# A sparse mixture of experts, split into two lots of tokens that are routed and combined beside other work

## The chip, the cores and the metric

The kernel runs on one core of a Trainium2 chip. Its time is the device time of one execution in microseconds (us). The core has a matrix engine (TensorE, called PE in the profile; its weight loads are shown apart as PEld), a vector engine (VectorE, DVE), an activation engine (ScalarE, ACT), a general engine (GpSimd, POOL) and a queue processor that issues most transfers (SyncE, SP). Each engine runs its own instructions in order; semaphores tie the engines together. 16 DMA engines move data between the large memory (DRAM) and the on-chip memory (SBUF); TensorE writes its results to a small accumulator memory (PSUM).

## The reference: what is computed

There are 4096 tokens of 256 numbers (`x`) and a sparse row-normalized 4096 x 4096 matrix (`adj`). Two layers, each made of a propagation over the graph and a mixture of experts:

```
x = x + mamba(layernorm(relu(adj @ layernorm(x) @ gcn_w + gcn_b)))
x = x + sum over the top 2 of 8 experts of w_e * (gelu(h @ W1[e] + b1[e]) @ W2[e] + b2[e])     h = layernorm(x)
f = tanh(adj * adj) * (adj > 0);  keep the 700 largest of each row of f
x = x + relu(f @ (tanh(layernorm(x) @ W_proj + b_proj) @ W_gcn) + b_gcn)
x = x + sum over the top 2 of 6 experts of w_e * expert_e(h)                                   h = layernorm(x)
```

In the last line, the router is a small network (256 to 128, relu, to 6 numbers, softmax); the weights of the two chosen experts are a softmax over their two values. An expert is three layers of 256 x 256 with relu behind the first two. Only two of the six experts count for a token, so the kernel computes only those: 8192 rows (token, expert) instead of 24,576. No row of `adj` in the given inputs has more than 22 entries, so "the 700 largest" keeps all of them.

## The kernel before

**Tokens.** They are held in 8 chunks of 512 (`NC`, `CW`), each 4 groups of 128 (`TPC`, `P`). `x3` is the result of the second propagation, all of it on chip.

**The second propagation** (`propagate1`) makes one chunk of 512 output rows after the other. Per chunk there are 16 steps: load a block of the transposed matrix (SP), relu (DVE, L1344), square and tanh (ACT, L1345, L1346), count the positive entries (DVE), and four matrix products into `pf` (L1355). At the end of the chunk, `pc` sums the counts (L1361), ACT applies relu, TensorE transposes back (`ps_ft`) and DVE adds into `x3`. A callback, `before(j2)`, puts other work between the steps. In chunk 0 it carries the combining of the first mixture and `node_features`; in chunks 1 to 7 it carries the routing of the chunk just finished: `prepare` at step 2, `choose` at step 6.

**Routing a chunk** (`Route`). `prepare` normalizes the chunk, stores the rows to DRAM (`d_xd`), transposes them, applies the router's first layer and computes the logits. `choose` picks the two experts as one-hot rows (`oh`), the two weights (`wv`), and each row's place within its expert (`place`, with running counts from chunk to chunk in `count`); `one_hot` then writes `lo`, a one-hot of the place modulo 128.

**The tables** (`tables`, L257). Rows of one expert are padded to tiles of 256 rows (`TR`), so every tile has one expert. 8192 rows and 6 experts need at most `K` = 37 tiles. `tables` inverts the map from row to place: for every batch of 8 groups DVE makes two one-hots over the `C` = 74 half tiles (`tb_hot`, `tb_eq`), and TensorE multiplies them with `lo` into `ps_inv` (L300; 64 products of 148 columns). From the sums DVE works out, per place, which row to fetch (`src`), the expert of each tile (`exps`), the tile's biases, and where the result goes (`dst`).

**The tiles** (`expert_tiles`, L421). For tile k, SP reads the expert's number into a register (`expert`) and loads three weight matrices (`wk`, three buffers each) and a bias; POOL fetches 2 x 128 rows by index (`xk`, L359, four buffers). TensorE transposes them (`ps_xt`, L465), DVE copies them to `xkT`, and TensorE runs the layers (`ps_h`, L444), with ACT between them (`hk`, L448). The last layer (`ps_y`, L429) of tile k stands behind the first layer of tile k+1; DVE adds the bias (`yk`, L434) and POOL scatters the rows by index to `d_ys` in DRAM (L367).

**Combining** (`combine`, L492). For a chunk, SP loads two blocks of 512 KB from `d_ys` (`yg`, three buffers; token t of group g, one row of 1 KB per partition and group), one with each token's first expert and one with its second. Both loads wait for the last four scatters. DVE does `dst = yg * weight + src` for 4 groups and both blocks (L503). For the second mixture the result goes to `x3`, and SP stores it to `out` (L1493).

**The order before.** After the propagation's 8 chunks, the kernel takes the largest count of a row (`most`) into a register; `If(many > TOPK)` holds an exact row-by-row top-700 and a new routing of 7 chunks, which these inputs don't need. Then come, one after the other: routing of chunk 7, `tables` for all rows, 37 tiles, and the combining of 8 chunks. The first mixture (8 experts) is built by the same functions; it runs 35 tiles, and up to 4 more in a branch of its own when the counts ask for them.

**What sets the order.** The program is written as one sequence; a static scheduler puts it on the engines' queues in that order. Pools of buffers add waits: an instruction that writes a buffer again waits for the last reader of what was in it. So the place of an instruction in the text, and the number of buffers, decide what is queued behind what.

Of the kernel before, what the change touches and what calls it, by code (L numbers as in the profile page):

```python
# [9 lines left out]
F32 = mybir.dt.float32  # L10
# [8 lines left out]
P = 128  # L19
# [4 lines left out]
TOPK = 700  # L24


@with_exitstack
def kernel(ctx: ExitStack, tc: tile.TileContext, out: bass.AP, **a):
# [122 lines left out]
    class Dispatch:  # L151
# [4 lines left out]
        def __init__(self, pool, E, name, batches):  # L156

            self.E, self.pool, self.name, self.T = E, pool, name, batches
            self.t0 = [sum(batches[:b]) for b in range(len(batches))]
            self.K = 2 * N // TR + E - 1  # L160
# [7 lines left out]
            self.xd = dram.tile([N, D], F32, name=f"{name}_xd")  # L168
            self.ys = dram.tile([2 * N + self.K * TR, D], F32, name=f"{name}_ys")
# [3 lines left out]
            self.oh = []  # L173
            for b, T in enumerate(batches):
                t = pool.tile([P, 2 * T + 1, E], BF16, name=f"{name}_oh{b}")
                nc.gpsimd.memset(t[:, :1, :], 0.0)
                self.oh.append(t)
# [8 lines left out]
            for i in range(2):  # L186
                nc.vector.tensor_scalar(
                    self.group[:, :, i], iota[:, :NT], float(i * NT), None, ALU.add
                )
# [12 lines left out]
        def place(self, b, psum, tag, pool):  # L202
# [6 lines left out]
            ps, tot = (psum.tile([P, CW], F32, name=f"ps_pl{i}", tag=tag) for i in range(2))  # L209
# [47 lines left out]
        def tables(self, psum, tp, biases):  # L257


            E, K, C, name = self.E, self.K, self.C, self.name  # L260
            nt = small.tile([P, E], F32, name="tb_nt", bufs=1)
# [10 lines left out]
            self.tiles = self.pool.tile([1, 1], I32, name=f"{name}_tiles")  # L272
            nc.vector.tensor_copy(self.tiles, ct[0:1, 0, E - 1:E])

            ps = psum.tile([P, CW], F32, name="ps_inv", tag="pl")
            group = self.group.rearrange("p t i -> p (t i)")
            shift = tp.tile([P, 2 * NT], F32, name="tb_shift", bufs=1)
            for b, T in enumerate(self.T):
                g0, G = 2 * self.t0[b], 2 * T
                one = tp.tile([P, G, E], F32, name=f"tb_one{G}")  # L280
                nc.vector.tensor_tensor(
                    one, self.oh[b][:, 1:, :], base.to_broadcast([P, G, E]), ALU.mult
                )
                nc.vector.tensor_reduce(shift[:, g0:g0 + G], one, AX.X, ALU.add)
            nc.vector.tensor_tensor(shift, shift, self.hi, ALU.add)
            S = 2 * TPC
            for g0 in range(0, 2 * NT, S):
                eq = tp.tile([P, 2, S, C], BF16, name="tb_eq", bufs=3)
                hot = tp.tile([P, S, C], BF16, name="tb_hot", bufs=3)
# [9 lines left out]
                for g in range(S):  # L299
                    nc.tensor.matmul(  # L300
                        ps[:, :2 * C], self.lo[:, g0 + g, :], eq[:, :, g, :],
                        start=(g0 + g == 0), stop=(g0 + g == 2 * NT - 1),
                    )

            tmp = tp.tile([P, K, E], F32, name="tb_tmp", bufs=1)
# [14 lines left out]
            grp = tp.tile([P, C], I32, name="tb_grp", bufs=1)  # L320
            no = tp.tile([P, C], F32, name="tb_no", bufs=1)
# [3 lines left out]
            nc.vector.tensor_scalar(grp, grp, NT - 1, None, ALU.bitwise_and)  # L325
# [5 lines left out]
            out = []  # L331
            for n, b in enumerate(biases):
# [9 lines left out]
                out.append(bk)  # L342

            nc.vector.scalar_tensor_tensor(
                tok, inv[:, 1, :], float(P), inv[:, 0, :], ALU.mult, ALU.add
            )
            nc.vector.tensor_scalar(tok, tok, -1.0, None, ALU.add)
            nc.vector.tensor_scalar(no, inv[:, 0, :], 0.0, None, ALU.is_equal)
            nc.vector.tensor_scalar(inv[:, 1, :], iota[:, :C], float(P), part1, ALU.mult, ALU.add)
            nc.vector.tensor_scalar(inv[:, 1, :], inv[:, 1, :], float(2 * N), None, ALU.add)  # L350
# [3 lines left out]
            return out  # L354
# [32 lines left out]
    class Route:  # L387
# [9 lines left out]
        def prepare(self, b):  # L397
            dp, E = self.dp, self.dp.E
            xn = self.pool.tile([P, TPC, D], F32, name="xn_r")
            layernorm(self.source[:, b * TPC:(b + 1) * TPC, :], xn)  # L400
# [20 lines left out]
    def expert_tiles(dp, psum, pool, weights, bias_out, layers, kb_out, spare):  # L421
# [3 lines left out]
        def finish(k, w, bk, hT):  # L425
# [25 lines left out]
        def tile_of(k, prev):  # L451
# [18 lines left out]
            for n, (mb, func, bias) in enumerate(layers):  # L470
                hT = layer(ws[n], hT, mb, func, bias[:, :, k:k + 1], f"hk{n}")
                if n == 0 and prev is not None:
                    finish(*prev)
            return k, ws[-1], bk, hT

        def run(first, last):
            prev = None
            for k in range(first, last):
                prev = tile_of(k, prev)
            finish(*prev)  # L480

        if not spare:
            return run(0, dp.K)


        most = 2 * N // TR + dp.E // 2 - 1
        tiles = nc.values_load(dp.tiles[0:1, 0:1], min_val=1, max_val=dp.K)
        run(0, most)
        with tc.If(tiles > most):
            run(most, dp.K)  # L490

    def combine(dp, pool, c, src, dst):  # L492

        yg = []
        for i in range(2):
            yg.append(pool.tile([P, TPC, D], F32, name="yg", bufs=3))
            ld = nc.sync.dma_start(yg[i], tokens(dp.ys, i * NC + c))
            for o in dp.sent[-4:]:
                after(ld, o)
        for t in range(TPC):  # L500
            s_ = c * TPC + t
            for i in range(2):
                nc.vector.scalar_tensor_tensor(  # L503
                    dst[:, s_, :], yg[i][:, t, :], dp.wv[:, s_, i:i + 1], (src, dst)[i][:, s_, :],
# [748 lines left out]
    with ExitStack() as s2:  # L1253
        with ExitStack() as st:
            tp = st.enter_context(tc.tile_pool(name="tiles0", bufs=2, reuse_waits="tile"))
            with ExitStack() as sr:
# [7 lines left out]
                (b1k,) = dp.tables(ps_r, rp, [b1])  # L1264
# [8 lines left out]
            expert_tiles(  # L1273
# [112 lines left out]
        def route_of(c):  # L1386
            def step(j2):
                if j2 == 2:
                    early.prepare(c)
                elif j2 == 6:  # L1390
                    early.choose(c)
# [169 lines left out]
```

## Time and profile before

| | |
|---|---|
| time before, median of 3 | 2511.99 us (2510.48 to 2512.32) |
| the profiled execution's own time | 2536.95 us |
| its span | 2535.2 us |
| TensorE busy, mean granted clock | 2262.7 us (89%), 0.946 |
| VectorE, ScalarE, GpSimd busy | 1652.5, 1194.7, 1137.6 us |
| bytes moved, mean rate | 507.85 MB, 200 GB/s |
| second propagation's last product into `pf` ends | 2193.2 us after the span's start |
| first layer of the first tile starts | 2246.66 |
| last tile's result added (`yk`) | 2485.64 |
| span ends | 2535.2 |

The page describes one execution by the hardware's profiler. A span is the time between its first and last instruction; the execution's own time is the span and a little around it. Engines are counted as busy while they execute, not while they wait. The granted clock is the share of full speed that the chip allowed TensorE in a stretch of time. In a "slices" view the span is cut into 40 equal parts and a digit is the busy share in tenths. In a "windows" view each line is a stretch, with the busy time of the engines, the clock, the share of time that the 16 DMA engines were busy (it may be slightly over 1) and the bytes per second. A "chain" follows the work that ended last from the end backwards, always to what released it. In a "timeline" line: start, duration, engine, line, operation, output <- inputs, shape, and in brackets how long the engine had idled and for what.

### The profile page before, as it was taken

The page shows a single profiled execution, that of the slowest core. Times are in us where ns is not written, and L with a number is a line of the kernel's source. Part 1 is how long each engine was busy: PE and PEld are TensorE (multiplying, and loading weights), DVE is VectorE, ACT ScalarE, POOL GpSimd, SP SyncE. Part 2 cuts the span into 40 slices and gives each one's busy share as a digit, 9 for nine tenths or more (in the row PEclk, how much of TensorE's full clock was granted, in tenths as well). Part 3 has the DMA queues.
Part 4 walks back from the last instruction along what each step waited for, and adds up shares of the span by engine and source line. Part 5 has one row for each costly group of instructions (what it writes and reads, how often), then busy time and mean ns, then how long its engine had stood idle before and what let it go on. Part 6 is the DMA issues. An engine that isn't in the chain of part 4 may idle for free. (4 is left out here: it accounts for less than half of the span.)

```text
span 2535.2 us, 25727 instructions
## 1 busy us (share of the span) xinstructions
PE 2262.7 (89%) x7996; PEld 1448.4 (57%) x7996; DVE 1652.5 (65%) x2324; ACT 1194.7 (47%) x2025; POOL 1137.6 (45%) x831
## 2 busy tenths in 40 slices
PE   5999999899999999897967999699999999769992
PEld 4765655656465656544636888555444444357781
DVE  4049999999999999988983111382666666432224
ACT  1146656574655566575722222244665656322330
POOL 1037676777777777765623555210000000036650
PEclk9989999999999999998978999899999999879996
DMA  6369999989899999996745777541444444147776
GB/s 200 92 179 225 241 271 233 266 227 270 222 271 230 250 256 238 263 244 195 237 148 175 236 229 232 192 150 59 153 151 147 147 148 145 47 146 224 231 228 215
DMA packets 302015, 507.85 MB, mean 200 GB/s; under 512 B 25248, under 2 KB 173728, under 8 KB 300976
## 3 DMA queue, kind: packets, MB, share of 16 engines
q1 hardware_dynamic: 255792, 409.63, 51.6%
q0 software_dynamic: 46080, 96.50, 18.0%
q8 instruction: 67, 1.10, 0.2%
q14 instruction: 76, 0.62, 0.1%
HBM read 404.85 MB, written 42.47 MB: 176 GB/s over the span
## 5 line engine op out<-in xcount | busy, mean ns | idle before, releaser
L1082 POOL TENSOR_TENSOR db<-du,bb 128x1024 f32<-128x1024 f32 x256 | 607.4, 2373 | 355.8 <-ACT state L1103 127.7
L1097 DVE TENSOR_TENSOR_SCAN db<-da,state,db 128x512 f32<-128x512 f32 x512 | 627.4, 1266 | 43.3 <-ACT da L1090 41.0
L621 PE MATMUL pt<-at,gn 128*128 128x256 f32 x2048 | 491.8, 393 | 35.9 <-DMA at<-in_adjT_dram 27.3
L1090 ACT ACTIVATE da<-dt,negA 128x512 f32<-128x512 f32 x512 | 347.8, 691 | 358.4 <-DVE db L1097 356.6
L621 PEld LDWEIGHTS pt<-at,gn 128*128 128x128 f32 x2048 | 400.8, 197 | 167.1 <-issue 74.0
L1355 PE MATMUL pf<-f,gn 128*128 128x512 f32 x1024 | 449.4, 594 | 0.0
L1124 PE MATMUL psy<-hc,ident 128*128 128x512 f32 x576 | 305.4, 624 | 42.6 <-DMA hc<-hc 36.3
L1107 DVE TENSOR_TENSOR hc<-db,cb 128x1024 f32<-128x1024 f32 x256 | 331.3, 1294 | 17.9
L1355 PEld LDWEIGHTS pf<-f,gn 128*128 128x128 f32 x1024 | 191.8, 190 | 227.3 <-issue 225.7
L448 ACT ACTIVATE hk<-ps_h,d_b 128x256 f32<-128x256 f32 x288 | 136.2, 474 | 380.3 <-PE ps_h L444 268.4
L434 DVE TENSOR_TENSOR yk<-ps_y,bk 128x512 f32<-128x512 f32 x72 | 49.8, 692 | 384.9 <-PE ps_y L429 288.7
L78 POOL TENSOR_TENSOR ln_rs<-ln_rs,mhalf 128x4 f32<-128x4 f32 x24 | 34.5, 1437 | 573.2 <-DVE ln_rs L77 573.2
L1345 ACT ACTIVATE f<-f 128x1024 f32<-128x1024 f32 x128 | 135.3, 1057 | 198.7 <-DVE f L1344 176.9
L359 POOL DMA_INDIRECT xk<-d_xd,d_src x144 | 140.2, 973 | 186.5 <-PE ps_xt L465 79.3
L429 PE MATMUL ps_y<-wk,hk 128*128 128x256 f32 x856 | 209.0, 381 | 7.9 <-issue 4.6
L444 PE MATMUL ps_h<-xkT,wk 128*128 128x256 f32 x856 | 209.3, 387 | 2.7 <-issue 2.4
L367 POOL DMA_INDIRECT d_ys<-yk,d_dst x144 | 142.4, 989 | 130.4 <-DVE yk L434 97.2
L1344 DVE TENSOR_SCALAR f<-at 128x1024 f32<-128x1024 f32 x128 | 88.1, 688 | 166.1 <-PE pf L1355 159.4
L1111 POOL DMA_DIRECT2D hc<-hc x224 | 195.5, 873 | 0.2
L1124 PEld LDWEIGHTS psy<-hc,ident 128*128 128x128 f32 x576 | 110.1, 198 | 119.9 <-issue 62.1
L444 PEld LDWEIGHTS ps_h<-xkT,wk 128*128 128x128 f32 x856 | 158.2, 192 | 35.6 <-ACT hk L448 9.4
L429 PEld LDWEIGHTS ps_y<-wk,hk 128*128 128x128 f32 x856 | 159.8, 190 | 30.8 <-issue 6.2
(236 smaller groups left out, 2491.7 us busy)
## 6 DMA issues: line engine op xcount, KB each, us to landing
at<-in_adjT_dram SPq DMA_DIRECT2D x256, 512.0 KB
bb<-bcd SPq DMA_DIRECT2D x128, 512.0 KB
cb<-bcd SPq DMA_DIRECT2D x128, 512.0 KB
hc<-hc POOLq DMA_DIRECT2D x224, 256.0 KB
wk<-in_L_ffn_W_dram SPq DMA_DIRECT2D x70, 512.0 KB
wk<-in_L_ffn_expert_w_dram SPq DMA_DIRECT2D x111, 256.0 KB
yg<-d_ys SPq DMA_DIRECT2D x32, 512.0 KB
yd<-us SPq DMA_DIRECT2D x6, 1024.0 KB
```

Of the source, the lines that this page charges most:

```text
L359: nc.gpsimd.indirect_dma_start(out=xk[:, j, :], out_offset=None, in_=self.xd[:, :], in_offset=bass.IndirectOffsetOnAxis(ap=self.src[:, c:c ...
L367: s_ = nc.gpsimd.indirect_dma_start(out=self.ys[:, :], out_offset=bass.IndirectOffsetOnAxis(ap=self.dst[:, c:c + 1], axis=0), in_=yk[:, j, ...
L429: nc.tensor.matmul(ps[:, j, :], hT[:, m, j * P:(j + 1) * P], w[:, m, :], start=(m == 0), stop=(m == kb_out - 1),)
L444: nc.tensor.matmul(ps[:, j, :], w[:, d, m * P:(m + 1) * P], xT[:, d, :], start=(d == 0), stop=(d == DB - 1),)
L621: nc.tensor.matmul(pt[:, k, :], xl[:, j, k * P:(k + 1) * P], at[:, jj, :], start=(j == 0 and k == 0), stop=(j == NT - 1 and k == DB - 1),)
L1082: nc.gpsimd.tensor_tensor(self.db, self.f.du[self.half][:, self.mi:self.mi + 1, :].to_broadcast([P, 2, CW]), self.bb, ALU.mult,)
L1090: nc.scalar.activation(da, self.f.dt[self.half][:, self.mi, :], AF.Exp, scale=negA[:, self.m, n:n + 1])
L1097: nc.vector.tensor_tensor_scan(self.db[:, j, :], da, self.db[:, j, :], state[:, self.m, n:n + 1], ALU.mult, ALU.add,)
L1107: nc.vector.tensor_tensor(self.hc, self.db, self.cb, ALU.mult)
L1111: nc.gpsimd.dma_start(self.hc[:, 0, :], self.hc[:, 1, :], accum_op=ALU.add)
L1124: nc.tensor.matmul(f.psy[m], ident, self.hc[:, j, :], start=False, stop=(self.g == GS - 1 and j == last),)
L1355: nc.tensor.matmul(pf[:, k, :], gn[:, j, k * P:(k + 1) * P], f[:, jj, :], start=(j == 0), stop=(j == NT - 1),)
```

## The change

The second mixture is done in two lots of tokens: lot a is chunks 0 to 5 (`SPLIT` = 6), lot b is chunks 6 and 7. Each has a `Dispatch` of its own, with its own counts, tables, `d_xd` and `d_ys`.

- Lot a needs at most K = 29 tiles and 27 are run; lot b at most 13, and 11 are run (`few`). That is 38 in place of 37.
- `tables` became a generator that stops after each batch. Lot a's tables are stepped from the callback in the last chunk of propagation, at every step but 2 and 6, where chunk 6 is routed as before. Its one-hots lie in the buffers that held `yg` of the first mixture, its sums in a buffer of `pf`.
- The branch between propagation and mixture is gone.
- A hook, `also(n)`, runs behind tile n of the 38. Behind tiles 1 to 26 it carries a piece each of chunk 7's routing and of lot b's tables, until they are done. Behind tiles 28, 29, 31, 32, 34 and 35 it carries the combining of one of lot a's six chunks and its store. Lot b's two chunks are combined after the last tile.
- `d_ys` has another row order: the four rows of a partition lie beside each other, so a load of `yg` takes 4 KB per partition in one piece. `dst` needs three more steps on DVE for it. The first mixture has this order too.
- A flag is set when a row has over 700 entries or when either lot needs more tiles than were run. `If(again > 0)` at the very end then does everything again in a general way (exact top-700 where it was, routing of 8 chunks, tables, all 37 tiles, combining).
- The one-hots of all batches of one size share a buffer, so `tables` treats them with one instruction each; the per-row offsets are summed from bf16 products.

```diff
+SPLIT = 6
...
-            self.K = 2 * N // TR + E - 1
+            self.NT = NT = sum(batches)
+            self.K = 2 * NT * P // TR + E - 1
...
-            self.ys = dram.tile([2 * N + self.K * TR, D], F32, name=f"{name}_ys")
+            self.S = 1 << (NT // TPC - 1).bit_length()
+            self.ys = dram.tile([2 * self.S * CW + self.K * TR, D], F32, name=f"{name}_ys")
...
-        def tables(self, psum, tp, biases):
+        def tables(self, ps, tp, biases, hots=None):
...
+            yield
             S = 2 * TPC
-            for g0 in range(0, 2 * NT, S):
-                eq = tp.tile([P, 2, S, C], BF16, name="tb_eq", bufs=3)
-                hot = tp.tile([P, S, C], BF16, name="tb_hot", bufs=3)
+            for g0 in range(0, NG, S):
+                eq = hots((P, 3, S, C))
+                hot = eq[:, 2]
...
+                yield
...
-    def expert_tiles(dp, psum, pool, weights, bias_out, layers, kb_out, spare):
+    def expert_tiles(jobs, psum, pool, weights, bias_out, layers, kb_out, also=None):
...
+        prev = None
+        for n, (d, k) in enumerate(jobs):
+            prev = tile_of(d, k, prev)
+            if also is not None:
+                also(n)
+        finish(*prev)
...
             yg.append(pool.tile([P, TPC, D], F32, name="yg", bufs=3))
-            ld = nc.sync.dma_start(yg[i], tokens(dp.ys, i * NC + c))
+            r0 = (i * dp.S + c) * CW
+            ld = nc.sync.dma_start(
+                yg[i], dp.ys[r0:r0 + CW, :].rearrange("(p t) d -> p t d", t=TPC)
+            )
...
         def route_of(c):
+            d = early[c >= SPLIT]
+            table = None
+            if c == NC - 2:
+                table = dp1[0].tables(
+                    ps_f.tile([P, DB, CW], F32, name="pf")[:, 0, :], tb, [eb1, eb2],
+                    lambda shape: wk.tile(list(shape), BF16, name="tb_eq", tag="yg", bufs=3),
+                )
             def step(j2):
                 if j2 == 2:
-                    early.prepare(c)
+                    d.prepare(c - d.dp.c0)
                 elif j2 == 6:
-                    early.choose(c)
+                    d.choose(c - d.dp.c0)
+                elif table is not None:
+                    next(table, None)
             return step
...
-    many = nc.values_load(mosti[0:1, 0:1], min_val=0, max_val=N)
...
-        with tc.If(many > TOPK):
...
+    def to_out(d, b, pool):
+        c = d.c0 + b
+        o = pool.tile([P, TPC, D], F32, name="oc")
+        combine(d, pool, b, x3[:, c * TPC:(c + 1) * TPC, :], o)
+        return nc.sync.dma_start(tokens(out, c), o)
+
+    few = [2 * d.NT * P // TR + E1 // 2 for d in dp1]
...
+        def routing():
+            late.prepare(NC - 1 - SPLIT)
+            yield
+            late.choose(NC - 1 - SPLIT)
+            yield
+            yield from dp1[1].tables(
+                ps_r.tile([P, CW], F32, name="ps_inv", tag="m"), rp, [eb1, eb2]
+            )
+
+        pieces = routing()
+        ready, op = list(range(SPLIT)), []
+
+        def also(n):
+            if n == few[0]:
+                assert next(pieces, None) is None
+                sr.close()
+                op.append(s4.enter_context(tc.tile_pool(name="out1", bufs=2, reuse_waits="tile")))
+            elif n < few[0]:
+                if n > 0:
+                    next(pieces, None)
+            elif (n - few[0]) % 3 != 0 and ready:
+                stores.append(to_out(dp1[0], ready.pop(0), op[0]))
+
+        tiles1([(d, k) for d, f in zip(dp1, few) for k in range(f)], psums, tp, also)
+        for b in range(NC - SPLIT):
+            stores.append(to_out(dp1[1], b, op[0]))
...
+        nc.vector.tensor_scalar(flag, flag, TOPK + 0.5, None, ALU.is_gt)
+        for d, f in zip(dp1, few):
+            nc.vector.scalar_tensor_tensor(flag, d.tiles, f + 0.5, flag, ALU.is_gt, ALU.add)
+        after(nc.vector.tensor_copy(flagi, flag), dp1[1].sent[-1])
+        again = nc.values_load(flagi[0:1, 0:1], min_val=0, max_val=3)
+    with tc.If(again > 0):
...
-            rt.prepare(NC - 1)
-            rt.choose(NC - 1)
-            b1k, b2k = dp1.tables(ps_r, rp, [eb1, eb2])
...
-        for c in range(NC):
-            combine(dp1, op, c, x3, x3)
-            nc.sync.dma_start(tokens(out, c), x3[:, c * TPC:(c + 1) * TPC, :])
```

## The prediction, made before the changed kernel was run

> **What bounds the kernel now.** I read the page's slices first, then the windows, then the chain of waits and the timeline over the last 340 us, where all the large edits lie.
>
> The slices, 63.4 us each; the last six are the second mixture:
>
> ```profile
> PE   5999999899999999897967999699999999769992
> PEclk9989999999999999998978999899999999879996
> DMA  6369999989899999996745777541444444147776
> ```
>
> TensorE is full except in two places near the end: where the second propagation gives way to the mixture (slices 35 and 36) and in the last slice. The windows (stretch, then PE, PEld, DVE, ACT and POOL busy, clock, DMA share, GB/s) show what fills them:
>
> ```profile
> 2131.90:2193.30 61.40, 61.13 (x162) 27.80 (x162) 37.53 (x79) 30.79 (x34) 1.85 (x1) 1.00 0.36 112
> ...
> 2210.00:2222.00 12.00, 0.31 (x2) 0.11 (x1) 10.95 (x65) 0.98 (x3) 0.00 (x0) 0.51 0.00 0
> 2234.00:2246.00 12.00, 1.86 (x6) 0.91 (x6) 5.04 (x20) 0.00 (x0) 7.80 (x9) 0.50 0.97 295
> ...
> 2320.00:2340.00 20.00, 19.95 (x97) 16.68 (x96) 5.44 (x8) 6.17 (x13) 12.57 (x13) 1.00 0.69 235
> ...
> 2504.00:2514.00 10.00, 0.00 (x0) 0.00 (x0) 7.07 (x18) 0.00 (x0) 0.00 (x0) 0.50 1.05 342
> ```
>
> Propagation is bound by PE (61.13 of 61.4) and leaves DVE 24 us a chunk. Then one engine after another works alone: DVE routes and builds tables, POOL starts the fetches, and the DMA queues load weights. In the tiles PE is full. In the tail PE does nothing and DMA is saturated.
>
> The chain names what ended last in the two gaps, and one tile's period between them:
>
> ```profile
> 2195.42 5.60 issue
> 2248.63 5.45 another core or an unknown queue
> 2282.22 1.99 PE ps_h L444 x8
> 2288.26 1.99 PE ps_h L444 x8
> 2490.43 3.95 DMA yg<-d_ys
> 2498.17 5.82 DMA yg<-d_ys
> ```
>
> The timeline gives the edges:
>
> ```profile
> 2193.13 0.59 PE L1361 MATMUL pc<-cnt,ones_b 128*1 128x512 bf16 x2
> 2202.10 1.38 DVE L80 TENSOR_SCALAR xn_r<-x,ln_mv,ln_rs 128x256 f32<-128x256 f32 x4 [1.12 <-POOL ln_rs L78]
> 2225.53 2.00 PE L300 MATMUL ps_inv<-tb_eq,d_lo 128*128 128x148 bf16 x16 [0.58 <-DVE tb_eq L295]
> 2246.66 1.92 PE L444 MATMUL ps_h<-xkT,wk 128*128 128x256 f32 x4
> 2485.64 0.69 DVE L434 TENSOR_TENSOR yk<-ps_y,bk 128x512 f32<-128x512 f32 x1 [3.99 <-PE ps_y L429]
> 2490.43 6.03 SPq L497 DMA_DIRECT2D yg<-d_ys  x4
> 2501.76 0.40 SPq L1493 DMA_DIRECT2D out_dram<-x  x1
> ```
>
> Propagation's last matmul ends at 2193.2, the first tile's first layer starts at 2246.66: a head of 53 us. The last tile's result is added at 2485.64, its scatter lands at 2490.3, the span ends at 2535.2: a tail of 45 us.
>
> **The change part by part**, in us of the profiled execution (span 2535.2, time 2536.95). The median of the runs shown is 2511.99, 25 us less; I carry differences over unscaled (1% of 40 us is 0.4).
>
> *Does the new fixed number of tiles suffice?* Lot a runs 27 tiles, lot b 11, and anything more goes to the general path. I computed the router's choices from the reference's inputs: lot a has 387, 1232, 858, 1845, 1182 and 640 rows, that is 2+5+4+8+5+3 = 27 tiles; lot b has 146, 384, 294, 621, 374 and 229, that is 11. Both fit with nothing to spare. The nearest count that could add a tile is 229, which would need 28 more rows, and the smallest gap between second and third logit is 4e-5, so rounding won't move it.
>
> *1. Lot a's tables inside the last chunk of propagation.* PE gets 48 table matmuls; 16 took 2.00 at 148 columns (now 116), so 6.0 at most, all on the path since PE is full there. DVE gets six pairs of one-hots (0.77 each at 592 columns, now 464, so about 7) and some 12 of small steps, 19 on top of 37.5: 57 in a chunk that now lasts 67. In the built order the last table step stands three matrix pieces before the end, so indices, fetches (six at 1.25) and weights are issued in the last 15 to 25 us of the chunk. The weight loads stand on SP's queue right after the last adjacency load and wait only for the table matmuls, whose buffers they reuse. Taken +6; bounds +4 (fewer columns scale fully) and +12 (DVE falls 6 behind).
>
> *2. The head.* The branch between propagation and mixture goes (x3's add ends at 2196.43, the next statistics start at 2198.95: 2.5), and so does the wait for routing, tables, fetch and weights. What stays on PE's queue, in built order: two tiles' transposes, then transposes of the last chunk's normalized rows, then the first layer. So PE still waits for that layernorm: 2202.10+0.41-2.5 = 2200.0, and starts the first layer about 2201.2. That is 45.5 earlier than 2246.66. Bounds: -47 (it need not wait for the copy) and -36 (it also waits for chunk 7's hidden layer and logits, 2202.66 to 2209.6 now, and the copies between).
>
> *3. Filling.* The first tiles now run at clock 0.66 and wait 5.45 for late weights. With weights there and PE hardly idle: -5 (0 to -6).
>
> *4. The last chunk's routing between tiles.* Chunk 6's same steps ran at full clock in 1.64 (transposes), 1.88, 0.95 and 0.5, plus 16 table matmuls 2.0: +7 of PE work. PE is in order, so it also waits where ACT or DVE is late (four places); behind it queue the tiles' matmuls. Only the exponentials-to-one-hot chain is long (2209.6 to 2213.4), and tile work stands between. Taken +10 (7 to 17).
>
> *5. One tile more.* 37 tiles took 2246.66 to 2485.6, 6.46 each: +6.5 (6.0, the undisturbed period 2282.22 to 2288.26, to 7).
>
> *6. Six chunks combined beside lot b's tiles.* New on SP's queue, ahead of later weights: 12 loads and 6 stores of 512 KB; on DVE 48 steps of 0.48 (3.85 a chunk, where yk and xkT take 1.4 of a tile's 6.04). Bytes: a tile moves 233 GB/s x 6.3 us = 1.47 MB, ten tiles 14.7 MB, the chunks 9.4 MB, 24.1 MB in all. At the tail's 342 GB/s that takes 70 us, at the tile stretch's 235/0.69 also 71; ten tiles take 63. So 8 from bytes. On top, SP stands for the last scatters of lot a and for DVE at each store, with the weights of two tiles ahead behind it; and DVE stands for a load while the next tile's xkT copy is queued behind (by the order I get about 5 for PE once, near lot b's fourth tile). Taken +15. Bounds: 0 (all hidden) and +28.5, six times the 4.75 that a chunk now costs in the tail, as if none of it overlapped.
>
> The Trainium skill (DMA: Bandwidth & Descriptors, Issuing engines are not separate DMA queues) says that DMAs of all issuers end up on the same 16 engines and interleave, so loads moved beside tiles aren't taken off them; and Specifications puts HBM at about 358 GB/s a core. By that figure the 24.1 MB take an estimated 67 us, the bytes' share of this step would be 4 instead of 8, and the whole -44 instead of -40. No row here reaches 358; the highest stretch is 342.
>
> *7. The tail.* Two chunks remain. From the scatter's landing at 2490.3, today's second store is issued at 2501.76 (11.5 later); the last DVE step ends at 2530.8, 4.4 before the end. So 15.9 instead of 44.9: -29. Loads of four rows per partition in one piece may be quicker; nothing shows it. Bounds -31 and -24 (loads at 5.82 rather than 3.95, twice, and a slow store).
>
> *8. The branch at the end* now jumps over the general path. Today's branch costs 2.5 to 5.6; most of it passes while the last store lands. +2 (0 to 5).
>
> *9. First mixture.* Table sums in bf16, three DVE steps more of 0.2, results read in the new row order: 0 (-3, as 16 loads stand at the start of a propagation chunk where PE idles 19.5 for the first; +1).
>
> Sum: 6 - 45.5 - 5 + 10 + 6.5 + 15 - 29 + 2 + 0 = **-40**. All bounds bad: +10.5; all good: -70.
>
> **The rivals.**
> - *More hidden than I think* (chance 0.13): step 6 costs the bytes' 8 or less, step 1 and 4 their lower bounds: 4-47-6+7+6+4-30+1 = -61, 2451. For it: the DMA share of a tile is only 0.69 to 0.78. Against: DVE and SP stand in order.
> - *The head stays half open* (0.14): PE's order puts routing ahead of tiles, DVE is late in the last chunk: 12-36-3+17+6.5+15-29+2 = -15.5, 2496. For it: four in-order waits on short chains. Against: DVE has 10 us to spare.
> - *Combining starves the tiles: slower* (0.09). Place: SP and DVE in lot b. If a chunk costs PE a loaded read (5.82), DVE's 3.25 and the two copies of a tile (1.4), 10.5 each, step 6 is 63 and the sum +8: 2520. It decides from 9.2 us a chunk ((40+15)/6). For it: the DMA share 1.05 in the tail. Against: weights are asked for two tiles (12 us) ahead.
> - *The general path runs* (0.01): at least 37 more tiles, 239 us, besides the row loop; ruled out by the counts unless these are wrong.
>
> **How the numbers follow.** My forecast, -40, has 0.60; 0.03 is left for a sum near nothing. Predicted: 2511.99-40 = 2472. Its own range is 2455 to 2489. To leave out no more than 2 in 10, I take in most of the first two rivals: 2446 to 2500. The measurement of this kernel can tell about 0.2% (5 us). Faster by more: 0.60+0.13+0.14 = 0.87; within: 0.03; slower: 0.09+0.01 = 0.10.
>
> **What would show it.** After: table matmuls among pf's in the last chunk, and that chunk about 67 long; the first ps_h within 10 us of the last pf; no wait of 5 for weights there; 38 tiles; lot b's tiles at 7 to 8 us against 6.0 to 6.5; yg loads of six chunks before the last scatter; the span ending about 16 to 18 after it lands. I'm wrong if lot b's tiles take 10 us or more, if PE idles over 15 us at the head, or if the matmuls of the general path appear.

## The result, and the profile after

The changed kernel takes 2477.72 us (median of 4, 2470.45 to 2479.38) where the kernel before, in the runs that go with it, takes 2512.15 (median of 4, 2510.48 to 2519.68). The ratio is 0.985, with a 95% interval of 0.982 to 0.988: 34 us, or 1.4%, faster. Predicted were 2472, with a range of 2446 to 2500.

One thing has to be known for all that follows. The kernel was later run on three more occasions, on three chips, and the kernel before took 2518.4 us on one of them, 2532.9 on another and 2536.2 on the last. I call them chips A, B and C. Times are therefore compared only with runs of the kernel before on the same chip. The changed kernel itself was run on A and not on B or C; a variant that ran there is set against the ratio of A. That a ratio holds from chip to chip was seen for one kernel only, the variant with "fetched rows in memory of their own" (0.9816 on A, 0.9821 on C). On chip A the two kernels stood side by side: 2477.85 against 2518.36, ratio 0.984 (0.983 to 0.986), 40.5 us. The execution of before that was profiled for the prediction took 2536.95 us, like those on B and C; the one profiled after took 2478.58, like those on A. The spans of these two profiles therefore differ by 58.5 us, more than the change is worth.

The stages, in us, from three profiles of before (the one shown, chip B, chip C) and two of after (the one on record, chip A):

| stage | before | after |
|---|---|---|
| start to the first product into `pf` | 1646.6, 1643.2, 1649.1 | 1651.7, 1650.0 |
| first to last product's end | 546.6, 546.4, 547.5 | 548.1, 549.4 |
| head: to the first tile's first layer | 53.5, 54.3, 54.1 | 11.1, 11.1 |
| to the last tile's result | 239.0, 235.4, 236.7 (37 tiles) | 243.2, 245.7 (38 tiles) |
| tail: to the end | 49.5, 49.1, 49.1 | 22.6, 22.7 |

Head and tail agree within 1 us in all traces of a kernel, and they carry the gain: some 43 and 27 us. The slices of the profile on record show it, 61.9 us each:

```profile
PE   5989989999999999896994999969999999989985
PEclk9989999999999999997996999989999999999998
DMA  6259898999999999988655777743344444447886
```

The first of the two thin places of before is gone: from the 28th slice, where the second propagation starts, no digit of PE is below 8 but the last, which holds the tail. The clock keeps its 9s through the change from propagation to mixture (slice 36), and from the 28th slice on DMA is now busiest in slices 38 and 39, lot b's. The windows of the same profile (stretch, then PE, PEld, DVE, ACT and POOL busy, clock, DMA share, GB/s):

```profile
2132.00:2199.90 67.90, 67.24 (x218) 31.31 (x217) 44.64 (x112) 34.18 (x39) 1.85 (x1) 1.00 0.42 132
2199.90:2211.00 11.10, 4.03 (x20) 2.43 (x19) 5.71 (x19) 1.26 (x2) 7.98 (x8) 0.78 0.29 72
2300.00:2320.00 20.00, 19.95 (x97) 16.67 (x96) 5.44 (x8) 6.32 (x14) 13.33 (x14) 1.00 0.78 240
2380.00:2400.00 20.00, 16.13 (x73) 12.94 (x72) 9.98 (x22) 4.27 (x9) 10.47 (x12) 0.93 0.89 299
2400.00:2420.00 20.00, 16.34 (x69) 13.48 (x69) 8.65 (x19) 4.75 (x11) 8.44 (x10) 0.90 0.94 315
2420.00:2440.00 20.00, 18.01 (x85) 14.14 (x84) 10.40 (x22) 5.69 (x12) 8.07 (x9) 1.00 0.99 323
2455.00:2466.00 11.00, 0.00 (x0) 0.00 (x0) 2.73 (x8) 0.00 (x0) 1.94 (x2) 0.67 0.54 190
```

Line 2 is the head: 11 us, in which PE works for 4. Line 3 is lot a's tiles alone, PE full. Lines 4 to 6 are lot b's tiles with lot a's chunks combined beside them: DMA goes from 0.78 to 0.99 and PE loses 2 to 4 us in every 20. The last line is the start of the tail.

What holds the head at 11 us is seen in the chain of waits of the same profile:

```profile
2199.89 1.28 ACT fT L1408 x2
...
2207.52 0.95 POOL xk L383
...
2208.49 1.07 POOL ln_rs L79
...
2209.58 0.42 DVE xn_r L81
...
2210.05 0.48 PE ps_tr L91
2210.52 0.64 PE ps_xt L491 x3
2211.16 1.71 PE ps_h L470 x4
```

Chunk 7's layernorm has one step on POOL (`ln_rs`), and it stands behind the row fetches of the first three tiles. DVE, then PE's transposes of the normalized rows (`ps_tr`), and behind these the first tile's layer wait for it. The fetches themselves are late. The timeline of POOL:

```profile
2201.16 1.03 POOL L383 DMA_INDIRECT xk<-d1a_xd,d1a_src  x1 [55.59 <-ACT fT L1408]
```

The indices they use are written at 2175.05, 26 us before. The fetch waited for `fT`, the propagation's last use of the memory that `xk` was given.

In lot b, the chain of waits shows both stops that the prediction named:

```profile
2385.57 5.18 DMA yg<-d1a_ys
...
2396.39 0.40 SPq L1470
...
2400.53 9.57 DMA wk<-in_L_ffn_expert_w_dram
...
2432.57 1.67 DVE oc L524 x4
2434.24 0.61 DVE xkT L495
2434.89 1.13 PE ps_h L470 x4
```

SP issues the store of a combined chunk (L1470) when DVE is done with it; the weights of a later tile stand behind it on SP's queue, go out at 2400.53, and need 9.57 us to land on full DMA queues. At 2432.57 the copy `xkT` stands behind a chunk's four combining steps, and PE's layer behind the copy.

### The profile page after: what moved, and what is told of

Its sections match the earlier page's. It is cut to its first block, busy times and chain, and to the rows that moved or that the text cites. A ratio compares the mean times of both kernels' runs of the same rounds, so it can differ in the third digit from the quotient of the medians.

```text
span 2476.7 us, 25809 instructions
## 1 busy us (share of the span) xinstructions
PE 2259.5 (91%) x8024; PEld 1448.7 (58%) x8024; DVE 1652.7 (67%) x2368; ACT 1194.0 (48%) x2029; POOL 1141.4 (46%) x830
## 5 line engine op out<-in xcount | busy, mean ns | idle before, releaser
L470 PE MATMUL ps_h<-xkT,wk 128*128 128x256 f32 x864 | 214.7, 390 | 12.5 <-DVE xkT L495 8.4
L474 ACT ACTIVATE hk<-ps_h,d_b 128x256 f32<-128x256 f32 x140 | 66.2, 474 | 184.2 <-PE ps_h L470 184.2
L1394 DVE SCALAR_TENSOR_TENSOR cnt<-at,cnt 128x1024 bf16<-128x1024 f32 x120 | 146.1, 1217 | 11.6 <-DMA at<-in_adjT_dram 10.5
L754 PE MATMUL ps_xz<-hT,w_in 128*128 128x512 f32 x256 | 126.4, 630 | 14.7 <-ACT hT L742 14.7
```

The lines of the kernel that those rows point to most:

```text
L470: nc.tensor.matmul(ps[:, j, :], w[:, d, m * P:(m + 1) * P], xT[:, d, :], start=(d == 0), stop=(d == DB - 1),)
L1394: nc.vector.scalar_tensor_tensor(cnt, at, 0.0, cnt, ALU.is_gt, ALU.add)
```

## The experiments

The theory was the prediction's: the head falls by the chain that is now hidden, the tail by six chunks, and lot b's tiles pay some 15 us for the combining beside them. The rivals were that combining beside the tiles hides little, that the head's parts cost in their new place what they cost in the old, and that the branch at the end costs more than it seems. All changes below are against the changed kernel, unless said otherwise.

### The changed kernel and the kernel before, again

> The changed kernel itself, measured beside the other variants, on the same chip as they. The runs so far come from two chips: before took 2512 on the one and 2533 on the other. Theory: the ratio to before is the same on both (0.985), so 2475 where before takes 2512, 2495 where it takes 2533, and where before's tiles of 5.2 us take 7.0 (every fifth), the same happens here. Rival: the change's gain is larger where the tiles have these stops: 0.980 or lower.

Chip A: 2477.85 (2477.08 to 2480.81) against 2518.36 for before; ratio 0.9842 (0.9826 to 0.9859). The ratio is the one on record, 0.985. In the trace of before, most results of the second mixture's tiles come 6.0 us after one another, but every fifth some 7.0 us; these are the stops that the expectation speaks of. Here, in lot a's tiles, every fifth result comes after 5.2 us, so the stops of 1.8 us are not there on this chip.

> The kernel before, unchanged, profiled a second time. The profiled execution of before took 2536.95 us where its unprofiled runs took 2512; the two profiles differ by 58.5 us in span, the medians by 34.4. Theory A: that one execution was slow by chance in the mixture's tiles (37 tiles in 239 us, PE idle for 14 of them, waits called issue of 1.2 us in every fifth tile), and a second profile has a span near 2510 to 2515, with its tiles nearer 225. Theory B: the profile itself or the kernel always costs this, and the span is again near 2535 with the same waits; then the runs without a profile differ in a way no trace shows.

Chip B: 2530.14, span 2528.4, and the same stops in every fifth tile. This is nearer to theory B: the stops are no chance of one execution.

> The kernel before once more, for a trace of it where its time is near 2512 to 2518: its two traces so far are from executions of 2530 and 2537. Theory: on such a chip every fifth tile of the second mixture takes 5.2 us as in the traces of the changed kernel there, in place of 7.0, so its 37 tiles take 225 to 230 in place of 235 to 239; head (54) and tail (49) are the same. Rival: the tiles take 235 or more there too, and the 15 us between the chips lie elsewhere.

This came to chip C, 2538.29, with the stops in every fifth tile once more. No trace of before was had on chip A, so the question was not answered directly; the section on the hardware has an answer from another kernel that ran on both A and C.

### Combining at the end, first in the text only, then held there

```diff
-            elif (n - few[0]) % 3 != 0 and ready:
-                stores.append(to_out(dp1[0], ready.pop(0), op[0]))
...
+        for b in range(SPLIT):
+            stores.append(to_out(dp1[0], b, op[0]))
         for b in range(NC - SPLIT):
             stores.append(to_out(dp1[1], b, op[0]))
```

> The changed kernel with one part undone: lot a's six chunks are combined after the last tile, followed by lot b's two. My theory (combining beside tiles hides most of it, step 6 against step 7 of the prediction): the tiles of lot b lose the stops that the trace of after shows (PE idle for 10.3 of 71.3 us), so -7 to -10, and the tail grows by six chunks at 4.75, +28.5; together +18 to +22 against after, 2496 to 2500, and the tail about 51 instead of 22.5. Rival (combining starves the tiles, so moving it there gains next to nothing): at most +5, with lot b's eleven tiles back from 71 to 50 or less than 47. Second rival (loads of four rows in one piece make a chunk cheaper in the tail than before, 3.9 or less): +13 to +16.

Chip B: 2495.18 (2492.77 to 2496.93), ratio 0.9856 (0.9836 to 0.9876), not to be told from the changed kernel's 0.9842. The tail is 22.7, not 51. The run told nothing of the price: the scheduler does not keep to the text and had put the six chunks back among lot b's tiles. (What is said of the order ahead of the prediction, that work is put on the queues in the order of the text, is too simple: waits and readiness let later work move forward.) So the loads were held by a dependency:

```diff
-            for o in dp.sent[-4:]:
+            for o in dp.sent[-4:] + list(late):
                 after(ld, o)
...
+            stores.append(to_out(dp1[0], b, op[0], dp1[1].sent[-4:]))
```

> The changed kernel with lot a's six chunks held back by a dependency: their loads wait for lot b's last scatter too, so that the scheduler can't put them among the tiles, as it did in the variant that only moved them in the text. My theory: the eleven tiles of lot b take 66 to 69 us from lot a's last result to the last, in place of 71 to 76 (-5 to -8), the tail grows by 4.75 for each of six chunks (+28.5): +20 to +24 against the changed kernel beside it. Rival (combining beside starves the tiles, so it hides little): +8 or less. Second rival (four rows in one piece are quicker: 3.9 a chunk): +15 to +18.

Chip A, beside the changed kernel: 2496.67 (2494.1 to 2499.01) against 2477.85, +18.8; ratio to before 0.9917 (0.9901 to 0.9932). The expectations that lie nearest, +20 to +24 and +15 to +18, can't be told apart by the two ratios, whose intervals allow 13 to 25; the traces decide. The two profiled executions differ by 14.6. In their traces the 38 tiles take 230.5 us in place of 245.7, so combining beside the tiles costs them 15.2; the tail takes 52.3 in place of 22.7, so it saves 29.6, or 4.9 a chunk. Windows of this variant, lot b's tiles and the tail:

```profile
2398.00:2418.00 20.00, 19.96 (x96) 16.73 (x95) 4.05 (x6) 6.72 (x15) 12.07 (x13) 1.00 0.84 257
...
2455.00:2475.00 20.00, 0.00 (x0) 0.00 (x0) 14.05 (x35) 0.00 (x0) 0.00 (x0) 0.50 0.96 324
```

PE is full in lot b's tiles (19.96 of 20), and the bytes go out in the tail at 324 GB/s, where lot b reached 323 in the changed kernel. Half of what is hidden is paid for. The rival that combining starves the tiles (+8 or less) falls, and so does the one that four rows in one piece are quicker: 4.9 a chunk here, 4.75 before.

### Lot a's tables behind the propagation

```diff
-            if c == NC - 2:
+            if c == NC:
...
             propagate1(c, route_of(c - 1) if c > 0 else features_of)
+        for _ in dp1[0].tables(
+            ps_f.tile([P, DB, CW], F32, name="pf")[:, 0, :], tb, [eb1, eb2],
+            lambda shape: wk.tile(list(shape), BF16, name="tb_eq", tag="yg", bufs=3),
+        ):
+            pass
```

> The changed kernel with one part undone: lot a's tables are made behind the propagation's last chunk, not between its steps. My theory (steps 1 and 2): the last chunk gets shorter by 6 to 7, and the head gets longer by the chain of the tables (19.5 from place to indices before, at 74 half tiles; 14 to 16 at 58), fetch, first transposes (6.2) and late weights, less what chunk 7's routing hides: 27 to 32 from the last product to the first layer in place of 11. Together +8 to +15: 2486 to 2493. Rival (the tables cost in the last chunk what they save): -3 to +3. Rival (fetches and weights behind the tables also fill more slowly): +20 or more.

Chip B: 2498.35 (2495.8 to 2501.45), ratio 0.9863 (0.9843 to 0.9883), against 0.9842 (0.9826 to 0.9859): about +5, but the intervals overlap. The traces are plainer, though they too come from two chips. The last chunk takes 61.8 us from `fT` to `fT` in place of 64.1 (-2.3), and the head 22.0 in place of 11.1 (+10.9): +8.6. The head was expected at 27 to 32; why it is shorter was not shown. A part of chunk 7's routing runs in it on PE, ahead of the first tile's layer, so it overlaps with the tables more than thought, it seems.

### Chunk 7's routing ahead of the tiles, in the text, then held there

```diff
         pieces = routing()
+        for _ in pieces:
+            pass
```

> The changed kernel with one part undone: routing of chunk 7 and lot b's tables stand ahead of the first tile, not between tiles. Lot a's tables stay in the last chunk. My theory (steps 2 and 4): PE's queue holds them ahead of the tiles, so PE waits for routing (2196.4 to 2213.4 before: 17) and for two batches of tables (about 6 to 8); what PE does between tiles today (5 to 7, with its waits 8 to 10) goes. Together +12 to +18: 2490 to 2496. Rival (the tiles between are PE-bound, the chain is hidden either way by the scheduler, which puts the first tile's work ahead): 0 to +4.

Chip B: 2489.01 (2483.44 to 2499.2), ratio 0.9825 (0.9806 to 0.9845): no loss. It says little, as the variant that moved the combining in the text alone: the first layer of the first tile still starts 11.8 us after the last product, among the routing. With a dependency on top:

```diff
+            self.made = nc.vector.tensor_copy(self.dst, tok)
...
+                if (self.name, k) == ("d1a", 0):
+                    after(ld, dp1[1].made)
```

> The changed kernel with routing of chunk 7 and lot b's tables held ahead of the tiles by a dependency (the first fetch waits for lot b's last table entry); moving them in the text alone had left the scheduler free to put the first tiles beside them. Lot a's tables stay in the last chunk. My theory (steps 2 and 4): head of 36 to 42 us in place of 11 (routing 17, two batches of tables 6 to 8, fetch and first transposes 6, first copy 1), the tiles beside lose 8 to 10: together +16 to +22 against the changed kernel (ratio to before 0.991 to 0.993). Rival (what stands between the tiles costs them as much as it would cost in front): +3 or less (0.985). Second rival (PE's filling slows too, with a low clock after the idle head): +25 or more (0.994).

Chip C: 2522.37 (2517.48 to 2528.69), ratio 0.9941 (0.9921 to 0.9961): 0.0099 more than the changed kernel on chip A, or 25 us. The head is 40.2 us, as expected (36 to 42), 29 more than 11.1. The windows of the head and of the first tile, up to its result:

```profile
2206.30:2246.50 40.20, 12.84 (x57) 6.89 (x56) 19.13 (x102) 4.38 (x9) 7.68 (x8) 0.59 0.24 65
2246.50:2262.50 16.00, 12.40 (x41) 9.80 (x41) 1.38 (x2) 2.73 (x6) 6.68 (x8) 0.74 0.34 99
```

The first tile needs 16.0 us to its result, at a clock of 0.74; in the changed kernel 9.3 and 9.9. So the head's 29 and the slower start's 6 are paid (3.7 of the start is a wait of ACT for something that the profile doesn't name, as in step 3 below). What is won back where routing left the tiles is 4.8 by chip A's traces (step 4 below). On chip C it is 12.7, against the kernel with fetched rows in memory of their own: from the first result to the 27th tile's that one needs 176.7, this one 164.0. That makes 22 to 30, and the ratios say 25, give or take 7. The second rival, filling that slows too, is the nearest, but the interval takes in the theory's 0.993.

### The end without branch

```diff
-        flag = small.tile([1, 1], F32, name="flag", bufs=1)
...
-    with tc.If(again > 0):
...
```

> The changed kernel without the flag, the branch and the general path at the end (for other inputs it would be wrong). Theory (step 8, taken +2, bounds 0 to 5): the branch passes beside the last stores, so -2 to 0. Rival: the end waits for the branch on all engines after the last store, or its code slows the fetching of instructions: -4 to -8.

Chip A: 2475.52 (2472.18 to 2480.36), 2.3 less than the changed kernel; ratio 0.9832 (0.9814 to 0.9851), which overlaps. In the traces the tail is 19.4 in place of 22.7. So 2 to 3 us; the time alone could not tell it from nothing.

### Fetched rows in memory of their own

```diff
+        xp = ctx.enter_context(tc.tile_pool(name="xk1", bufs=1, reuse_waits="tile"))
...
-        adp = s2.enter_context(tc.tile_pool(name="adj1", bufs=4, reuse_waits="tile"))
+        adp = s2.enter_context(tc.tile_pool(name="adj1", bufs=3, reuse_waits="tile"))
...
-            xk = pool.tile([P, 2, D], F32, name="xk", bufs=4)
+            xk = (xpool or pool).tile([P, 2, D], F32, name="xk", bufs=4)
...
+                if (self.name, k) == ("d1a", 4):
+                    after(ld, late.power)
```

> The changed kernel with the fetched rows (four buffers of 2 KB a partition) in memory of their own, for which the propagation's adjacency buffers go from 4 to 3, and POOL's step of chunk 7's layernorm placed ahead of the fetch of tile 4. The trace of after shows the first fetch at 2201.16, 26 us after its indices, held until the propagation's last use of that memory (fT), and the layernorm step at 2208.49 behind six fetches. Theory: the head's 11 us from the last product to the first layer becomes 4 to 5, PE's wait of 2.9 for chunk 7's normalized rows is gone: -6 to -9. Rival (the head is set by the weights or by chunk 7's own chain, or three adjacency buffers slow the propagation): -2 to +3.

Chip A: 2470.44 (2468.37 to 2474.13), 7.4 less than the changed kernel beside it, whose fastest run is 2477.08; ratio to before 0.9816 (0.9798 to 0.9834). The head is 4.8 us. The timeline of POOL in this variant:

```profile
2173.28 1.03 POOL L384 DMA_INDIRECT xk<-d1a_xd,d1a_src  x1 [30.44 <-DMA at<-in_adjT_dram]
...
2203.55 1.04 POOL L79 TENSOR_TENSOR ln_rs<-ln_rs,mhalf 128x4 f32<-128x4 f32 x1 [17.79 <-DVE ln_rs L78]
```

Eight fetches go out inside the last chunk, from 2173.28 on, and the layernorm step runs as soon as DVE has its input. The theory holds, and this kernel beats both. The variant makes two changes at once, so how much of the 7.4 is the memory's and how much the layernorm step's place was not separated.

> The kernel with fetched rows in memory of their own, again, beside the others of this call. Theory: the same ratio to before as measured first, 0.9816 (within 0.0015). Rival: that gain of 7 us was a matter of the chip or of the placement of memory, and the ratio is the changed kernel's 0.985.

Chip C: 2490.95 (2484.87 to 2496.56) against 2536.2, ratio 0.9821 (0.9797 to 0.9845). The ratio came again.

> Two edits that helped or looked better, together: fetched rows in memory of their own with the layernorm step ahead (as measured before, -7.4), and the combining of lot a's chunks left to the scheduler behind the last tile, which spreads it over more tiles: in that variant's trace the last eleven tiles took 68.2 us, in the changed kernel's traces 71.2 and 73.2. Theory: -3 to -5 against the kernel with the first edit alone, 0.980 of before. Rival (the bytes set the pace of lot b, wherever they stand): -1 to +1. Second rival (last chunks slip behind the last tile): +2 to +5.

It joins the edits of the variants "fetched rows in memory of their own" and "combining at the end, in the text only". Chip C, beside the kernel with the first edit alone: 2490.25 (2486.55 to 2492.7) against 2490.95. The rival holds: spread over the tiles in another way, the same bytes cost the same. With the 0.99 of DMA in lot b this speaks for the bytes as the limit there; it doesn't show it.

## Why the prediction was right, step by step

The time came within 6 us of the forecast, and on chip A the difference was the forecast's 40. Some of its terms were off, and they cancel: steps 1 and 4 were taken 8.5 us too dear together, step 2 was 2 to 3 too good, and step 9 left out 3 to 5. That the sum came so near is in part luck. Measured from the traces on record and on chip A, with all three traces of before:

| step | taken | measured |
|---|---|---|
| 1 lot a's tables in the last chunk | +6 (+4 to +12) | +2.7 |
| 2 head | -45.5 (-47 to -36) | -42 to -43 |
| 3 filling | -5 (0 to -6) | -4 to -7, between unlike chips |
| 4 routing between tiles | +10 (+7 to +17) | +4.8 |
| 5 one tile more | +6.5 | +5.9 |
| 6 combining beside lot b | +15 (0 to +28.5) | +15.2 |
| 7 and 8 tail and branch | -27 | -27 |
| 9 first mixture | 0 (-3 to +1) | +4 to +6, less 1 |

*Step 1 was mis-sized.* The table products were priced from a row at about half clock. Two windows of before, each around one batch of 16 products, and the timeline of PE after:

```profile
2225.53:2227.53 2.00, 2.00 (x16) 1.81 (x16) 2.00 (x4) 0.73 (x2) 0.00 (x0) 0.57 0.03 8
2228.27:2229.64 1.37, 1.37 (x16) 0.99 (x16) 1.37 (x3) 0.14 (x1) 0.00 (x0) 1.00 0.00 0
```

```profile
2140.59 0.57 PE L317 MATMUL pf<-tb_eq,d_lo 128*128 128x116 bf16 x8
2141.00 4.51 PE L1398 MATMUL pf<-f,gn 128*128 128x512 f32 x10
```

The batch that gave the price, 2.00 us, ran at a granted clock of 0.57; the next one, at 1.00, took 1.37, with a short pause in it. In the last chunk the clock is 1.00, and eight products hold the propagation's next one back for 0.41 us, so 16 cost 0.82 and all 48 cost 2.5 in place of 6.0. The columns (116 for 148) account for 0.78 of the price, and 0.82 of 2.00 is 0.41; the 0.52 that is left is the clock's. VectorE's part, taken as 19 us, was 6.4: it is busy for 43.95 us of the last chunk (2135.8 to 2199.9), where the prediction's window of before has 37.53. From `fT` to `fT` the last chunk takes 64.1 us and the others about 61.4. The Trainium skill (TensorE: Matmul & The Clock Gate, Part 1) has this rule: TensorE's clock is halved once it has idled for some microseconds, and full again only after a few of sustained work. The profile agrees: the clock is 0.51 in the prediction's window in which PE works for 0.31 of 12 us, and 1.00 in the busy last chunk. A row taken from such a stretch has to be scaled by the clock before it is moved into a busy one. The statement that indices and weights come in the last 15 to 25 us was right (indices at 2175.05), for the fetches it was wrong: they waited for memory.

*Step 2 was right in kind.* PE does wait for chunk 7's normalized rows, after two tiles' transposes. The time of it was wrong by 3 us (8.0 from the last product to the first layer, where 11.1 came), since the step moved the fetches into the last chunk and left POOL out of the chain: the layernorm's one step there stood behind six fetches of 1.25 us. That variants with the tables or the routing moved back have heads of 22.0 and 40.2 says what hides where: 11 us of the head went into the last chunk, 29 between the tiles.

*Step 3 came out in its number, but its reason was misread.* From the first layer to the first result it is 14.4 us in the trace shown before (13.9 and 16.5 in the other two), 9.3 and 9.9 after. The prediction took the wait of 5.45 in the chain for late weights. Before's timelines of SP, PE and ACT:

```profile
2232.32 1.53 SPq L458 DMA_DIRECT2D wk<-in_L_ffn_expert_w_dram  x3
...
2251.14 0.59 PE L444 MATMUL ps_h<-hk,wk 128*128 128x256 f32 x2
...
2254.11 0.47 ACT L448 ACTIVATE hk<-ps_h,d_b 128x256 f32<-128x256 f32 x1 [5.02 <-remote]
2254.63 1.22 PE L444 MATMUL ps_h<-hk,wk 128*128 128x256 f32 x2 [2.47 <-ACT hk L448]
```

The second layer already runs at 2251.14, so its weights are there. Then PE stands 2.47 us for an activation step, and this step, which reads no weights, waits for something that the profile does not name (`remote`). All three traces of before have this wait of 4.4 to 5.0 there; the two of after have none. But these come from unlike chips: in the variant with fetched rows in memory of their own, the second result comes 9.0 us after the first on chip A and 13.5 on chip C. So how much of the 4 to 7 the change brought, and how much the chip, stays open.

*Step 4 was mis-sized.* The 16 table products, taken as 2.0, have 52 columns here and run at a clock of 1.00: PE is busy with them for 0.9 us at most. And the in-order waits that it feared on PE didn't come: from 2220 to 2377 the view of PE's waits lists none. From the first result to the 27th tile's there are 26 intervals, 157.5 us together, where 26 undisturbed ones, 29.37 us for every five, take 152.7.

*Steps 6 to 8 were right,* the first to 0.2 us, which is luck. The estimate of the bytes (8 us) and of the stops in order (7) can't be told apart in one number; PE's waits in lot b of the profile on record (us in total, times, longest) are

```profile
PE ps_h L470 <- DVE xkT L495: 5.4, 2, 3.8
PE ps_h L470 <- DVE oc L524: 3.6, 1, 3.6
PE ps_h L470 <- ACT hk L474: 0.9, 2, 0.6
```

*Step 9 was wrong.* The first mixture's 34 intervals between results took 246.7 us in all three traces of before, and 252.3 and 250.7 in those of after. The change puts the pools of the propagation in another order, so that the adjacency buffers lie where memory comes free early. In the trace of before the propagation's first load is issued at 1624.64, after the mixture's tiles; in that of after four are issued between 1363.57 and 1378.58, between the weights of the first tiles. The first load on SP's queue, before and then after:

```profile
1624.64 0.89 SPq L1338 DMA_DIRECT2D at<-in_adjT_dram  x2
```

```profile
1363.57 0.38 SPq L1381 DMA_DIRECT2D at<-in_adjT_dram  x1
```

DVE's timeline after:

```profile
1387.44 0.69 DVE L1387 TENSOR_SCALAR f<-at 128x1024 f32<-128x1024 f32 x1 [6.86 <-DMA at<-in_adjT_dram]
1388.05 0.69 DVE L460 TENSOR_TENSOR yk<-ps_y,bk 128x512 f32<-128x512 f32 x1
1388.65 0.68 DVE L495 COPY xkT<-ps_xt 128x512 f32<-128x512 f32 x1
```

DVE stands 6.86 us for such a load, with the mixture's `yk` and `xkT` behind it, and the interval between two tiles' results becomes 11.8 in place of 7.4. The propagation's first chunk wins back 1.0 to 1.4. The prediction named the pools' order nowhere. That it is this order, and not the merged instructions of the tables, is argued from the traces; no run undid it alone.

The measured terms add up to between -40 and -45; the time moved by 34 (on record) and by 40.5 (chip A). They leave the stops out: the intervals between results of before's 37 tiles hold 10 to 14 us more than undisturbed ones would, which is why the tiles' row in the table of stages grows by 4 to 10 only, where steps 3 to 6 make 19 to 22. As no trace of before was had on a chip like A, what is left of the difference to the time on record stays open.

The rival that the general path runs is out: 54 fetches of lot a and 22 of lot b make 27 and 11 tiles, and nothing behind the branch appears in the trace.

## What to carry to other kernels

A serial chain that is put beside other work saves its latency, but what remains is found in the queues it shares: follow each of its instructions on every engine, and ask of each buffer which earlier work held its memory. Price moved products at the clock of the place they move to. When an experiment moves work in a program that a scheduler orders, hold it with a dependency, or look at where it went before reading the time; and when pools are reordered, look for loads that now start early.

## What the runs showed of the hardware that was not expected

The same kernel (fetched rows in memory of their own) took 2470.44 us on chip A and 2490.95 on chip C. In the two traces the spans are 2468.6 and 2489.0, and 18.4 of these 20.4 us lie in the second mixture's tiles (243.8 and 262.2). In both traces most tiles take 6.0 us. Every fifth tile has no transposes between its products, and takes 5.2 on A and 7.0 or 7.1 on C; the kernel before on B and C has 7.0 too. ACT in one such tile, on chip A and then on chip C, and PE behind it on C:

```profile
2283.36 0.47 ACT L477 ACTIVATE hk<-ps_h,d1a_b 128x256 f32<-128x256 f32 x1 [0.33 <-PE ps_h L473]
```

```profile
2300.52 0.47 ACT L477 ACTIVATE hk<-ps_h,d1a_b 128x256 f32<-128x256 f32 x1 [2.33 <-PE ps_h L473]
2301.05 1.56 PE L458 MATMUL ps_y<-wk,hk 128*128 128x256 f32 x6 [1.24 <-issue]
```

The same step starts after 0.33 us on A and after 2.33 on C, and PE has to wait. The waits of ACT from the end of the propagation to the last tile, on chip A and then on chip C (us in total, times, longest):

```profile
ACT hk L477 <- PE ps_h L473: 167.6, 149, 7.9
```

```profile
ACT hk L477 <- PE ps_h L473: 113.4, 88, 4.5
ACT hk L477 <- issue: 49.5, 39, 3.8
ACT hk L477 <- remote: 14.8, 7, 3.3
```

The 49.5 us under `issue` (nothing that the profile names) are not lost as a whole: most of these waits are of 1.22 us, as long as those that on chip A stand under PE in tiles of the same 6.0 us. What costs is the late step in every fifth tile, and a few waits of 2 to 4 us. This fits the 14.5 and 17.8 us by which the kernel before is quicker on chip A than on B and C. What holds ACT was not found out.
